# A selective scan on one Trainium2 core: dt * x copied into PSUM by ScalarE, u in PSUM, decays in SBUF three tiles ahead

## The chip, the cores and the metric

The kernel is one program on 1 core of one Trainium2 chip. The metric is the device time of one execution in microseconds (us), as the median of the runs. The core's engines work side by side, each on its own queue of instructions, and wait for one another through semaphores: PE (TensorE, matrix multiplications), DVE (VectorE), ACT (ScalarE), POOL (GpSimd) and SP (SyncE, which here issues all the DMA transfers). SBUF is the large on-chip memory, PSUM the small one of eight banks that PE writes its results to.

## What is computed

The reference runs four layers over 8 images of 56 x 56 positions and 128 channels. Layers 0, 2 and 3 are deformable convolutions with an MLP. Layer 1, the only one that the change touches, is a "visual state space" layer (SS2D): a normalization, a projection to 256 channels and a gate, a 3 x 3 convolution per channel, then a selective scan over the 3136 positions in K = 4 directions with N = 16 states per channel, and after it a normalization, the gate, a projection and an MLP. Of it the scan matters here:

```python
dt = jax.nn.softplus(dt + dt_projs_b[None, :, :, None])
A = -jnp.exp(A_logs).reshape(K, Di, N)

def step(h, t):
    dt_t, u_t, B_t, C_t = t
    h = h * jnp.exp(dt_t[..., None] * A) + (dt_t * u_t)[..., None] * B_t[:, :, None, :]
    y = jnp.einsum('bkdn,bkn->bkd', h, C_t)
    return (h, y)
...
_, ys = jax.lax.scan(step, h0, ts)
```

So for each channel and state there is a decay exp(dt * A), an input (dt * x) * B, a running sum h of decayed inputs, and the output, the sum over the states of h * C.

## The kernel before

**Steps and tiles.** The scan stage of the kernel (`Vss.scans`) goes through 8 images x 4 directions x 4 pieces of 784 positions (SC) = 128 steps. Each step has 32 tiles. A tile (the code's t) holds 32 channels x 4 states on the 128 partitions, and 784 positions; its channel group is cg (8 of them) and its state group sg (0 to 3). All four tiles of one channel group share the load `dt` [128, 2, 784] from DRAM: half 0 is dt, half 1 is dt * x, each channel's row repeated on its four states' partitions. The rows of B and C (`b`, `c`) are loaded once a step and state group. In all there are 4096 tiles and 1024 channel groups.

**One tile.** The operations, with the lines of the profile:

- `spread` (L1340), once per channel group: PE copies dt * x into the PSUM tile `dtu` by multiplying with the identity matrix. There is one buffer of two banks.
- `decay` (L1346): ScalarE writes dA = exp(dt * A) into PSUM, `dA`, two buffers of two banks each.
- `inputs`: for sg = 0, 1, 2 VectorE computes u = dtu * b (L1356) from PSUM into SBUF, `u`, two buffers. For sg = 3 (`on_pool`) GpSimd computes it from SBUF (L1352) into `up`, one buffer.
- the scan (L1449): VectorE's tensor_tensor_scan, h = dA * h + u along the 784 positions, into SBUF, three buffers.
- the state copy (L1452): ScalarE keeps h's last column in `st` for the direction's next piece (not for the last piece).
- `hc` (L1454): GpSimd computes h * c, six buffers.
- `add_sums` (L1378): PE sums over the four states into the PSUM tile `acc`, two tiles at a time and some tiles later; `open_sums` (L1370) and `close_sums` (L1389, ScalarE) begin and end a sum.

VectorE thus does three u and four scans for each channel group, and GpSimd four hc and one up.

**Beside the tiles** run background stages, written as generators that are advanced one piece at a time: `prepare` makes the next step's dt, dt * x, B and C (PE, ScalarE, and two GpSimd operations for each half of the channels), `input_stage` the next image's projections and convolution, `output_stage` the layer's end (with a Gelu or Silu on ScalarE between two loads of its function tables). All matrix results of these go through one PSUM bank, `misc`.

**Order.** In the loop, tile `now` writes down: background pieces, the decay and the u of tile now + 1, at sg = 1 the `spread` of the next channel group, then its own scan, state copy and hc. The tile framework then orders each engine's instructions when the program is built, by a plan of its own with that order as priority, assigns the buffers and adds the semaphore waits. On the chip each engine's queue is in order. `issue_after` puts the state sums behind the last `spread` on PE.

**Memory.** All eight PSUM banks are used: misc 1, dtu 2, dA 2 x 2, acc 1.

Of the kernel before, what the change touches and what calls it, by code (L numbers as in the profile page):

```python
# [41 lines left out]
F32 = mybir.dt.float32  # L42
BF16 = mybir.dt.bfloat16
I32 = mybir.dt.int32
AF = mybir.ActivationFunctionType
ALU = mybir.AluOpType
AX = mybir.AxisListType
PSUM = bass.MemoryType.PSUM
# [70 lines left out]
SC, SR = 784, 14  # L119
NSC = L // SC  # L120
SH = SC // 2
# [11 lines left out]
TC, TS = 32, 4  # L133
NCG, NSG = DI // TC, NST // TS
# [342 lines left out]
class Dcn:  # L477
# [9 lines left out]
    def run(self):  # L487
        tc, nc = self.tc, self.nc
        with ExitStack() as ctx:
            enter = ctx.enter_context  # L490
            self.cp = enter(tc.tile_pool(name="c_const", bufs=1))
            self.img = enter(tc.tile_pool(name="c_img", bufs=1))
            self.fp = enter(tc.tile_pool(name="c_front", bufs=1))
            self.up = enter(tc.tile_pool(name="c_unit", bufs=1))
            self.bp = enter(tc.tile_pool(name="c_block", bufs=3))
            self.tp = enter(tc.tile_pool(name="c_tail", bufs=1))
            self.pt = enter(tc.tile_pool(name="c_pt", bufs=3, space=PSUM))
            self.py = enter(tc.tile_pool(name="c_py", bufs=2, space=PSUM))
            self.pm = enter(tc.tile_pool(name="c_pm", bufs=3, space=PSUM))
            self.w = self.net.dcn_weights(self.layer, self.const)  # L500
            self.constants()
            self.split_bias()
            self.loop()
            self.check()
        over = nc.values_load(self.net.flag[:1, :1], min_val=0, max_val=1, skip_runtime_bounds_check_because="a comparison's result")
        with tc.If(over > 0):
            self.net.dcn_slow(self.layer, self.images, self.src, self.dst)
# [479 lines left out]
        nc.vector.tensor_scalar(net.flag, most, 0.0, None, ALU.is_gt)  # L987


class Vss:  # L990


# [6 lines left out]
    def run(self):  # L999
        tc = self.tc  # L1000
        with ExitStack() as ctx:
            enter = ctx.enter_context
            self.cp = enter(tc.tile_pool(name="v_const", bufs=1))
            self.img = enter(tc.tile_pool(name="v_img", bufs=1))
            self.prep = enter(tc.tile_pool(name="v_prep", bufs=1))
            self.work = enter(tc.tile_pool(name="v_work", bufs=2))
            self.bg = enter(tc.tile_pool(name="v_bg", bufs=1))
            self.dram = enter(tc.tile_pool(name="v_dram", bufs=2, space=DRAM))
            self.pmisc = enter(tc.tile_pool(name="v_misc", bufs=1, space=PSUM))
            self.pdtu = enter(tc.tile_pool(name="v_pdtu", bufs=1, space=PSUM))  # L1010
            self.pda = enter(tc.tile_pool(name="v_pda", bufs=2, space=PSUM))
            self.pacc = enter(tc.tile_pool(name="v_pacc", bufs=1, space=PSUM))
            self.weights()
            self.scans()
# [285 lines left out]
    def scans(self):  # L1300
        nc, w = self.nc, self.w
# [6 lines left out]
        units = [(at, t) for at in range(len(steps)) for t in range(NT)]  # L1308
# [22 lines left out]
        def on_pool(t):  # L1331

            return order[t][1] == NSG - 1

        def spread(at, t):

            s, (cg, sg) = state[at], order[t]
            ps = s["dtu", cg] = self.pdtu.tile([128, 2, 512], F32, name="dtu", tag="dtu")
            for b in range(2):
                last = nc.tensor.matmul(ps[:, b, :SH], lhsT=self.net.ident, rhs=s["dt", cg][:, 1, SH * b : SH * (b + 1)], start=True, stop=True)  # L1340
            self.last_spread = last.ins

        def decay(at, t):
            (i, k, c), s, (cg, sg) = steps[at], state[at], order[t]
            da = s["dA", t] = self.pda.tile([128, 1024], F32, name="dA", tag="dA")
            nc.scalar.activation(da[:, :SC], s["dt", cg][:, 0], AF.Exp, scale=w["A"][:, k, NSG * cg + sg : NSG * cg + sg + 1])  # L1346

        def inputs(at, t):
            s, (cg, sg) = state[at], order[t]
            if on_pool(t):  # L1350
                u = self.work.tile([128, SC], F32, name="up", tag="up", bufs=1)
                nc.gpsimd.tensor_mul(u, s["dt", cg][:, 1], s["b", sg])  # L1352
            else:
                u = self.work.tile([128, SC], F32, name="u", tag="u", bufs=2)
                halves = [v.rearrange("p (x e) -> p x e", x=2) for v in (u, s["b", sg])]
                nc.vector.tensor_mul(halves[0], s["dtu", cg][:, :, :SH], halves[1])  # L1356
            s["u", t] = u
# [13 lines left out]

        def add_sums(at, group):
            acc = state[at]["acc"]
            with self.tc.issue_after(self.last_spread):
                for (cg, sg), hc in group:
                    for b in range(2):
                        r = 64 * b + TC * (cg % 2)
                        nc.tensor.matmul(acc[r : r + TC, :SH], lhsT=w["sum"], rhs=hc[:, SH * b : SH * (b + 1)], start=False, stop=sg == NSG - 1)  # L1378

        def close_sums(at, t):  # L1380
            (i, k, c), acc, (h, r) = steps[at], state[at]["acc"], place(t)
# [15 lines left out]
                    tasks.extend(self.output_stage(i, e) for e in (2 * c + 1, 2 * c))  # L1397

        spread(*units[0])
        decay(*units[0])  # L1400
        inputs(*units[0])
        st = ready = None
        group, late = [], deque()
        zeros = self.zeros()
        for now, (at, t) in enumerate(units):
            (i, k, c), s, (cg, sg) = steps[at], state[at], order[t]
            forward = k < 2
            if t == 0:
                if at % NSC == 0:
                    st = self.prep.tile([128, NT], F32, name="st", tag="st", bufs=2)  # L1410
                    nc.gpsimd.memset(st, 0.0)
                if at % (NDIR * NSC) == 0 and i + 1 < self.images:
                    tasks.append(self.input_stage(i + 1))
                ready = iter(())
                if at + 1 < len(steps):
                    if steps[at + 1][0] > i:
                        self.load_xb(i + 1)
                    ready = self.prepare(state[at + 1], *steps[at + 1][1:])
            if t % (2 * NSG) == 0:
                late.append((now + 5, open_sums, (at, t)))  # L1420
            while late and late[0][0] <= now:
                _, do, args = late.popleft()
                do(*args)
            if t % 2 == 0:
                next(ready, None)

            if sg == 1:
                to = divmod(NCG * at + cg + 2, NCG)
                if to[0] < len(steps):
                    self.fetch_dt(state[to[0]], to[1])  # L1430
            if t in (3, 19):
                next(zeros, None)

            for x, when in enumerate(((25, 28, 29, 30), (26, 29, 30, 31))):
                if t in when and at + 1 < len(steps):
                    self.fetch_row(state[at + 1], x, when.index(t))
            if now + 1 < len(units):
                decay(*units[now + 1])
                if not on_pool(units[now + 1][1]):
                    inputs(*units[now + 1])  # L1440

                if sg == NSG - 3 and now + 3 < len(units):
                    spread(*units[now + 3])
            if now + 2 < len(units) and on_pool(units[now + 2][1]):
                inputs(*units[now + 2])
            hh = self.work.tile([128, SC], F32, name="h", tag="h", bufs=3)
            step = 1 if forward else -1
            u, dA = s.pop(("u", t)), s.pop(("dA", t))
            nc.vector.tensor_tensor_scan(hh[:, ::step], dA[:, :SC][:, ::step], u[:, ::step], st[:, t : t + 1], ALU.mult, ALU.add)  # L1449
            if c != (NSC - 1 if forward else 0):  # L1450
                last = SC - 1 if forward else 0
                nc.scalar.copy(st[:, t : t + 1], hh[:, last : last + 1])  # L1452
            hc = self.work.tile([128, SC], F32, name="hc", tag="hc", bufs=6)
            nc.gpsimd.tensor_mul(hc, hh, s["c", sg])  # L1454
            group.append((order[t], hc))
            if t % 2:
                late.append((now + 3, add_sums, (at, group)))
                group = []
                if t % (2 * NSG) == 2 * NSG - 1:
                    late.append((now + 5, close_sums, (at, t)))  # L1460
            if t % 2 or t % 4 == 0 or (i == self.images - 1 and k == 2):
                advance(1)
# [81 lines left out]
```

## Time and profile before

| what | value |
|---|---|
| median of 3 runs | 18469.42 us (18464.81 to 18477.36) |
| profiled execution, span | 18479.8 us |
| the scan stage in it, first to last scan | 2376 to 13812 us, 11436 us |
| busy over the whole span: PE, DVE, ACT, POOL | 13780.6, 15510.8, 11145.4, 11801.5 us |
| busy in the scan stage: PE, DVE, ACT, POOL | 8635.2, 10255.6, 7049.6, 10451.1 us |
| granted TensorE clock, mean | 0.826 |

The profile is of one execution. The span counts from the first to the last instruction, and has no launch around it; it is 10.4 us above the median of the timed runs. A row of the profile's groups names a line of the kernel, an engine, the operation, what it writes and reads, how often it ran, its busy time and the mean of one in ns, and behind the last bar the idle time of that engine ahead of it with what ended most of that idle time. In a row of the timeline stand the start and the duration of one instruction; the last part of an instruction can overlap the next one's start on the same engine.

### The profile page before, as it was taken

How to read it: one execution, taken by the hardware profiler on the slowest of the kernel's cores; microseconds unless marked ns; L12 is line 12 of the kernel's file. 1: busy time of each engine (PE TensorE's matmuls, PEld its weight loads, DVE VectorE, ACT ScalarE, POOL GpSimd, SP SyncE). 2: the span in 40 equal slices, each digit the busy share in tenths (PEclk: the TensorE clock that was granted, in tenths of full speed). 3: DMA queues.
4: the chain of work that ended last, by engine and by line, in shares of the span. 5: the costliest groups of instructions: out<-in, count | busy, mean ns of one | idle time of the engine just before them, and what ended most of it. 6: DMA issues, size and time to landing. Idle time of an engine off the chain costs nothing. (4 is left out here: it accounts for less than half of the span.)

```text
span 18479.8 us, 257190 instructions
## 1 busy us (share of the span) xinstructions
PE 13780.6 (75%) x89795; PEld 6844.2 (37%) x89795; DVE 15510.8 (84%) x18797; ACT 11145.4 (60%) x20690; POOL 11801.5 (64%) x6462
## 2 busy tenths in 40 slices
PE   5777787678678778678778768767665888577777
PEld 4555422222222222222222222222224666455555
DVE  8888379988988988988988898898985887688886
ACT  4666565566566566566566656656554666456666
POOL 2221089998998998998998998899981111222221
PEclk7878888889889889889888888888886888677777
DMA  7777444444443444344343443443433777577777
GB/s 215 205 210 200 122 158 160 162 158 148 142 149 137 146 147 140 140 150 139 140 150 136 143 152 135 143 150 136 147 122 110 196 198 198 143 204 204 201 204 175
DMA packets 1341779, 2961.90 MB, mean 160 GB/s; under 512 B 91168, under 2 KB 892132, under 8 KB 1325836
## 3 DMA queue, kind: packets, MB, share of 16 engines
q1 hardware_dynamic: 1340460, 2945.21, 51.4%
q8 instruction: 718, 11.76, 0.3%
q14 instruction: 601, 4.92, 0.1%
HBM read 2243.88 MB, written 866.92 MB: 168 GB/s over the span
## 5 line engine op out<-in xcount | busy, mean ns | idle before, releaser
L1454 POOL TENSOR_TENSOR hc<-h,c 128x784 f32<-128x784 f32 x4096 | 7560.9, 1873 | 764.2 <-DVE h L1449 534.4
L1449 DVE TENSOR_TENSOR_SCAN h<-dA,st,u 128x784 f32<-128x784 f32 x3072 | 5569.9, 1838 | 316.2 <-ACT dA L1346 182.3
L1346 ACT ACTIVATE dA<-dt,v_A 128x784 f32<-128x784 f32 x4096 | 3742.8, 915 | 719.1 <-DVE h L1449 717.8
L1356 DVE TENSOR_TENSOR u<-dtu,b 128x784 f32<-128x784 f32 x3072 | 2875.7, 957 | 559.9 <-PE dtu L1340 555.5
L1378 PE MATMUL acc<-hc,v_sum 128*32 128x392 f32 x16384 | 3222.3, 552 | 105.8 <-POOL hc L1454 105.6
L1340 PE MATMUL dtu<-dt,ident 128*128 128x392 f32 x4096 | 2105.1, 642 | 1512.1 <-issue 1102.6
L736 POOL TENSOR_TENSOR ay<-hat,om 112x756 f32<-112x756 f32 (+2 forms) x192 | 525.8, 2738 | 2750.0 <-ACT hat L727 2346.6
L1449 DVE TENSOR_TENSOR_SCAN h<-dA,st,up 128x784 f32<-128x784 f32 x1024 | 1876.7, 1833 | 242.4 <-POOL hc L1454 176.7
L1352 POOL TENSOR_TENSOR up<-dt,b 128x784 f32<-128x784 f32 x1024 | 1900.3, 1856 | 132.1 <-DVE h L1449 110.8
L807 ACT COPY st<-pt 128x448 f32<-128x448 f32 (+1 forms) x2240 | 1177.8, 542 | 1216.4 <-PE pt L805 1210.1
L1452 ACT COPY st<-h 128x1 f32<-128x1 f32 x3072 | 581.7, 189 | 2159.0 <-DVE h L1449 2150.5
L1340 PEld LDWEIGHTS dtu<-dt,ident 128*128 128x128 f32 x4096 | 862.0, 235 | 2564.6 <-issue 1672.2
L775 DVE TENSOR_TENSOR win<-win,patch 112x252 f32 (+2 forms) x3456 | 1695.4, 503 | 124.4 <-DVE win L775 34.2
L805 PE MATMUL pt<-ident,sw 112*128 112x112 f32 (+2 forms) x8960 | 1609.7, 310 | 199.1 <-DMA sw<-skew 198.8
L1378 PEld LDWEIGHTS acc<-hc,v_sum 128*32 128x32 f32 x16384 | 769.8, 117 | 2488.2 <-issue 1675.4
L766 POOL MEMSET win<- 128x1820 f32 (+2 forms) x384 | 630.1, 1646 | 1466.2 <-DMA skew<-win 1159.6
L821 PE MATMUL yps<-st,xw 128*32 128x48 f32 (+5 forms) x35840 | 1077.7, 245 | 397.6 <-ACT st L807 394.8
L805 PEld LDWEIGHTS pt<-ident,sw 112*128 112x128 f32 (+2 forms) x8960 | 1119.5, 161 | 485.6 <-DMA sw<-skew 166.9
L772 DVE TENSOR_TENSOR patch<-ay,hat 112x756 f32<-112x756 f32 (+2 forms) x1152 | 1221.3, 1066 | 22.5 <-POOL ay L736 19.5
L821 PEld LDWEIGHTS yps<-st,xw 128*32 128x32 f32 (+2 forms) x35840 | 757.0, 126 | 825.9 <-ACT st L807 476.1
L1112 PE MATMUL misc<-xn,v_tap 128*128 128x448 f32 x2016 | 867.3, 574 | 96.5 <-ACT xn L1146 61.2
L725 ACT ACTIVATE hat<-om,taps 112x252 f32<-112x252 f32 x1280 | 755.7, 729 | 287.1 <-DVE patch L772 273.4
(165 smaller groups left out, 19517.2 us busy)
## 6 DMA issues: line engine op xcount, KB each, us to landing
dt<-dds SPq DMA_DIRECT2D x1024, 784.0 KB
b<-rows SPq DMA_DIRECT2D x512, 392.0 KB
c<-rows SPq DMA_DIRECT2D x512, 392.0 KB
dds<-dd SPq DMA_DIRECT2D x256, 784.0 KB
sw<-skew SPq DMA_DIRECT2D x224, 812.0 KB
sw<-skew SPq DMA_DIRECT2D x224, 672.0 KB
sw<-skew SPq DMA_DIRECT2D x224, 588.0 KB
xw<-table SPq DMA_DIRECT2D x224, 320.0 KB
```

What stands on the lines that cost most here:

```text
L772: nc.vector.tensor_mul(patch[:n], bcast(a, 3, KX), bcast(b, 2, KY))
L775: self.last_add = nc.vector.tensor_add(to, to, patch[:n, NCB * p : NCB * (p + 1)]).ins
L805: last = nc.tensor.transpose(ps[:m, n * g : n * (g + 1)], sw[:n, g, p : p + m], self.net.ident[:n, :n])
L807: nc.scalar.copy(st[:m], ps[:m, : G * n])
L821: self.nc.tensor.matmul(yps[CG * g : CG * (g + 1), t0:t1], lhsT=xw[:m, k + part, CG * g : CG * (g + 1)], rhs=st[:m, at + t0 : at + t1], st ...
L1340: last = nc.tensor.matmul(ps[:, b, :SH], lhsT=self.net.ident, rhs=s["dt", cg][:, 1, SH * b : SH * (b + 1)], start=True, stop=True)
L1346: nc.scalar.activation(da[:, :SC], s["dt", cg][:, 0], AF.Exp, scale=w["A"][:, k, NSG * cg + sg : NSG * cg + sg + 1])
L1352: nc.gpsimd.tensor_mul(u, s["dt", cg][:, 1], s["b", sg])
L1356: nc.vector.tensor_mul(halves[0], s["dtu", cg][:, :, :SH], halves[1])
L1378: nc.tensor.matmul(acc[r : r + TC, :SH], lhsT=w["sum"], rhs=hc[:, SH * b : SH * (b + 1)], start=False, stop=sg == NSG - 1)
L1449: nc.vector.tensor_tensor_scan(hh[:, ::step], dA[:, :SC][:, ::step], u[:, ::step], st[:, t : t + 1], ALU.mult, ALU.add)
L1454: nc.gpsimd.tensor_mul(hc, hh, s["c", sg])
```

## The change

- `spread`: a ScalarE copy of dt * x (both halves in one instruction) into `dtu` takes the place of the two identity matmuls, and is written down at sg = 2, for the next channel group, where it was at sg = 1. The state sums are no longer held behind it on PE.
- `decay`: for sg = 0, 1, 2 dA goes to SBUF, four buffers; for sg = 3 to PSUM, one buffer of its own (`dAp`). All are written down three tiles ahead (AHEAD) where it was one.
- `inputs`: VectorE's u goes to PSUM, one buffer of two banks, and is written down in its own tile just ahead of its scan, where it was one tile ahead in two SBUF buffers. GpSimd's `up` stays as it was, two tiles ahead.
- PSUM is again full: misc 1, dtu 2, dAp 2, u 2, acc 1.
- The scratch ring of descriptors for DMAs that GpSimd issues is set to 8192 bytes, half its size.

```diff
+AHEAD = 3
...
-            self.pda = enter(tc.tile_pool(name="v_pda", bufs=2, space=PSUM))
+            self.pda = enter(tc.tile_pool(name="v_pda", bufs=1, space=PSUM))
+            self.pu = enter(tc.tile_pool(name="v_pu", bufs=1, space=PSUM))
...
             ps = s["dtu", cg] = self.pdtu.tile([128, 2, 512], F32, name="dtu", tag="dtu")
-            for b in range(2):
-                last = nc.tensor.matmul(ps[:, b, :SH], lhsT=self.net.ident, rhs=s["dt", cg][:, 1, SH * b : SH * (b + 1)], start=True, stop=True)
-            self.last_spread = last.ins
+            nc.scalar.copy(ps[:, :, :SH], s["dt", cg][:, 1].rearrange("p (b e) -> p b e", b=2))
...
-            da = s["dA", t] = self.pda.tile([128, 1024], F32, name="dA", tag="dA")
-            nc.scalar.activation(da[:, :SC], s["dt", cg][:, 0], AF.Exp, scale=...)
+            if on_pool(t):
+                da = s["dA", t] = self.pda.tile([128, 1024], F32, name="dAp", tag="dAp")[:, :SC]
+            else:
+                da = s["dA", t] = self.work.tile([128, SC], F32, name="dA", tag="dA", bufs=4)
+            nc.scalar.activation(da, s["dt", cg][:, 0], AF.Exp, scale=...)
...
-                u = self.work.tile([128, SC], F32, name="u", tag="u", bufs=2)
+                u = self.pu.tile([128, 1024], F32, name="u", tag="u")[:, :SC]
...
-            with self.tc.issue_after(self.last_spread):
-                for (cg, sg), hc in group:
+            for (cg, sg), hc in group:
...
         spread(*units[0])
-        decay(*units[0])
-        inputs(*units[0])
+        for x in range(AHEAD):
+            decay(*units[x])
...
-            if now + 1 < len(units):
-                decay(*units[now + 1])
-                if not on_pool(units[now + 1][1]):
-                    inputs(*units[now + 1])
-
-                if sg == NSG - 3 and now + 3 < len(units):
-                    spread(*units[now + 3])
+            if now + AHEAD < len(units):
+                decay(*units[now + AHEAD])
+            if not on_pool(t):
+                inputs(at, t)
+            if sg == NSG - 2 and now + 2 < len(units):
+                spread(*units[now + 2])
             if now + 2 < len(units) and on_pool(units[now + 2][1]):
                 inputs(*units[now + 2])
...
-    nc = bacc.Bacc("TRN2", target_bir_lowering=False, num_devices=1)
+    nc = bacc.Bacc("TRN2", target_bir_lowering=False, num_devices=1, dynamic_dma_scratch_size=8192)
```

More of the change, by code (lines that the diff above doesn't have):

```diff
@@ L1338, in spread @@
             ps = s["dtu", cg] = self.pdtu.tile([128, 2, 512], F32, name="dtu", tag="dtu")
-            for b in range(2):
-                last = nc.tensor.matmul(ps[:, b, :SH], lhsT=self.net.ident, rhs=s["dt", cg][:, 1, SH * b : SH * (b + 1)], start=True, stop=True)
-            self.last_spread = last.ins
+            nc.scalar.copy(ps[:, :, :SH], s["dt", cg][:, 1].rearrange("p (b e) -> p b e", b=2))
         def decay(at, t):
             (i, k, c), s, (cg, sg) = steps[at], state[at], order[t]
-            da = s["dA", t] = self.pda.tile([128, 1024], F32, name="dA", tag="dA")
-            nc.scalar.activation(da[:, :SC], s["dt", cg][:, 0], AF.Exp, scale=w["A"][:, k, NSG * cg + sg : NSG * cg + sg + 1])
+            if on_pool(t):
+                da = s["dA", t] = self.pda.tile([128, 1024], F32, name="dAp", tag="dAp")[:, :SC]
+            else:
+                da = s["dA", t] = self.work.tile([128, SC], F32, name="dA", tag="dA", bufs=4)
+            nc.scalar.activation(da, s["dt", cg][:, 0], AF.Exp, scale=w["A"][:, k, NSG * cg + sg : NSG * cg + sg + 1])
         def inputs(at, t):
@@ L1373, in add_sums @@
             acc = state[at]["acc"]
-            with self.tc.issue_after(self.last_spread):
-                for (cg, sg), hc in group:
-                    for b in range(2):
-                        r = 64 * b + TC * (cg % 2)
-                        nc.tensor.matmul(acc[r : r + TC, :SH], lhsT=w["sum"], rhs=hc[:, SH * b : SH * (b + 1)], start=False, stop=sg == NSG - 1)
+            for (cg, sg), hc in group:
+                for b in range(2):
+                    r = 64 * b + TC * (cg % 2)
+                    nc.tensor.matmul(acc[r : r + TC, :SH], lhsT=w["sum"], rhs=hc[:, SH * b : SH * (b + 1)], start=False, stop=sg == NSG - 1)
         def close_sums(at, t):
@@ L1448, in scans @@
             u, dA = s.pop(("u", t)), s.pop(("dA", t))
-            nc.vector.tensor_tensor_scan(hh[:, ::step], dA[:, :SC][:, ::step], u[:, ::step], st[:, t : t + 1], ALU.mult, ALU.add)
+            nc.vector.tensor_tensor_scan(hh[:, ::step], dA[:, ::step], u[:, ::step], st[:, t : t + 1], ALU.mult, ALU.add)
             if c != (NSC - 1 if forward else 0):
```

## The prediction

> **What bounds the kernel now.** I read the busy time by stage first, then, for the scan stage alone, the groups by line, VectorE's waits, its timeline, and the critical chain's last pieces.
>
> The scan stage runs from the first scan at 2376 us to 13812 us, and all that the change touches lies in it:
>
> ```profile
> core 0: us, PE busy (x) PEld busy (x) DVE busy (x) ACT busy (x) POOL busy (x), PEclk, DMA share, GB/s
> 2376.00:13812.00 11436.00, 8635.16 (x31301) 3029.64 (x31300) 10255.58 (x8597) 7049.57 (x13024) 10451.07 (x5761) 0.86 0.41 145
> ```
>
> GpSimd is busy for 10451 of 11436 us and VectorE for 10256, so neither has 10% to spare; ScalarE has 4386 us free. The groups of that stage:
>
> ```profile
> L1454 POOL TENSOR_TENSOR hc<-h,c 128x784 f32<-128x784 f32 x4093 | 7555.5, 1873 | 761.2 <-DVE h L1449 531.4 <-PE acc L1378 176.1 <-DMA gate<-pre 13.4
> L1449 DVE TENSOR_TENSOR_SCAN h<-dA,st,u 128x784 f32<-128x784 f32 x3069 | 5564.4, 1838 | 316.1 <-ACT dA L1346 182.3 <-POOL hc L1454 37.7 <-issue 16.6
> L1346 ACT ACTIVATE dA<-dt,v_A 128x784 f32<-128x784 f32 x4090 | 3737.4, 915 | 719.1 <-DVE h L1449 717.8 <-ACT st L1452 0.5
> L1356 DVE TENSOR_TENSOR u<-dtu,b 128x784 f32<-128x784 f32 x3067 | 2871.1, 957 | 477.9 <-PE dtu L1340 473.5
> L1340 PE MATMUL dtu<-dt,ident 128*128 128x392 f32 x4088 | 2099.1, 642 | 1510.3 <-issue 1102.6 <-DVE u L1356 379.0 <-PE misc L1090 6.7
> ```
>
> GpSimd waits mostly for scans, scans for decays, u for dtu. VectorE's own longest waits:
>
> ```profile
> DVE u L1356 <- PE dtu L1340: 473.5, 258, 7.8
> DVE h L1449 <- ACT dA L1346: 234.3, 199, 4.2
> DVE h L1449 <- POOL hc L1454: 214.4, 165, 3.2
> ```
>
> (Total us, times, longest us.) VectorE's timeline shows a cost that is in no wait list:
>
> ```profile
> 8128.86 0.95 DVE L1356 TENSOR_TENSOR u<-dtu,b 128x784 f32<-128x784 f32 x1
> 8129.72 1.84 DVE L1449 TENSOR_TENSOR_SCAN h<-dA,st,u 128x784 f32<-128x784 f32 x1
> ...
> 8181.05 0.95 DVE L1356 TENSOR_TENSOR u<-dtu,b 128x784 f32<-128x784 f32 x1
> 8182.13 1.85 DVE L1449 TENSOR_TENSOR_SCAN h<-dA,st,u 128x784 f32<-128x784 f32 x1
> ```
>
> At 8129.72 a scan follows a u that it does not need: it starts 0.86 us after that u, before u's 0.95 us are over. At 8182.13 it needs the u just ahead: 1.08 us. Over the stage's VectorE rows the overlap of independent pairs is 0.084 us, and the gap where a scan takes the u just ahead 0.133 us: 0.217 us dearer. Where an instruction has only VectorE's own predecessor to wait for (the convolution chain of L637, the layer norm's last operations) the gap is 0.035 us, 0.118 us dearer.
>
> **The change part by part.** The sum is made against the profiled span, 18479.8 us; the median of the runs, 18469.4, lies 10.4 below it, which I take off at the end.
>
> *dtu from ScalarE.* 4096 matmuls of 642 ns (2099 us of PE) and their weight loads go, and 1024 copies come to ScalarE. The nearest rows are the two plain 128x784 operations of L1268 and L1269, 855 and 848 ns, and the decay, 915 ns: 0.85 us each, 870 us in all, so ScalarE goes from 7050 to 7920 us, 69% of the stage. The 473 us of VectorE waiting for dtu go, and what is late next is ScalarE itself. The copy can start when the group's third u is done; VectorE then has a scan and the GpSimd-fed scan to do, 3.6 us, so the copy must begin within 2.65 us. How late ScalarE is for something VectorE has just released can be read from the state copy L1452: of 3072 it began over 2.65 us after its scan's end in 224, and the excess is 86 us per 1024. With 12% more on the engine I take 100 (ends: 0, and the present 473). Net -373. Behind the waiting copy ScalarE holds the next decays, the state copies and the background stages; the decays are ahead, so I charge nothing more here, and the second rival prices it.
>
> *Decays three tiles ahead.* VectorE's 234 us for dA nearly vanish: three tiles are some 8 us of cover, and the longest wait was 4.2. I leave 30 (ends 0 and 234): net -204. Writing SBUF instead of PSUM costs ScalarE at most some 0.03 us per decay (855 without a per-partition scale against 915 with one into PSUM), off the path. The dt buffers are both released and needed two tiles earlier; a dt load lands in 4.7 us median, 14.1 at worst of 500, against some 11 us or more: nothing. The fourth decay keeps one PSUM buffer, free when the previous GpSimd-fed scan ends, a group earlier: nothing.
>
> *u in one PSUM buffer, issued beside its scan.* This is the cost. Now u may run ahead, as two SBUF buffers allow; the commonest order between two GpSimd-fed scans is u u scan scan u scan (565 of 1024 groups), with one direct hand-off. With one buffer u must be followed by its scan, and the next u may not start before that scan has read the buffer: u waits on VectorE's own semaphore for this today too, only two scans back. So 3072 hand-offs u to scan at 0.217 us, and 2048 from scan to u at 0.118 us (the first u of a group has the GpSimd-fed scan between). Background operations stand behind u in 15% of cases and behind a scan in 6% today; I let them hide as much: 567 + 227 = 794 us. Already paid: 565 x 0.217 + 106 x 0.118 = 135. Net +659 (ends: 0, and 774 with nothing hidden). The Trainium skill, "VectorE: DVE Perf Modes", section "The DRAIN you can't avoid", says that a chain of copies with a semaphore after each took as long as one with a semaphore at the end; by it this term would be 0 and the sum some 17,890. The 0.86 and 1.08 us above disagree, and I go by them.
>
> *u's duration.* No VectorE operation in this trace writes PSUM. Nearest rows: the statistics operation reading PSUM (417 ns for 256 columns) and SBUF (270 for 128) differ by some 13 ns once their slope is out; at the far end, the convolution's 128x784 all in SBUF is 1057 ns against u's 957. I take +13 ns x 3072 = +40 us, ends -307 and +307. The scan keeps one PSUM and one SBUF operand, exchanged: nothing. "Perfetto Trace Analysis", section "Optimizing Scalar/DVE Operations", gives VectorE about 60 ns of overhead per instruction on SBUF and 125 on PSUM, which speaks against moving u; by it the term would be an estimated 200 us. No run here shows it yet.
>
> *The rest.* VectorE's 218 us for GpSimd (hc and up) come in bursts when GpSimd prepares the next step, which stays: -30 (ends -218 and 0). Its 99 us for PE in background operations (48 statistics, 51 residual adds) profit from the freed PE: -15 (ends -99 and 0). The ring: every DMA was issued from SP and all of its packets are hardware_dynamic, so a smaller GpSimd ring is touched by nothing: 0; only the slow fallback path, which has no row, would use it.
>
> Sum: -373 - 204 + 659 + 40 - 30 - 15 = +77; 18479.8 + 77 - 10.4 = 18546.
>
> **The rivals.** The forecast is a small difference of two large terms, so I give the other ways much room. A measurement of this kernel tells some 0.2%, 37 us, from no change: 18432 to 18507 counts as the same.
>
> *Faster: the hand-off hardly costs.* With dA ready early, the GpSimd-fed scan may be planned between a u and its scan, and a hand-off through PSUM may be quicker than through SBUF. For it: the planner already moves u's freely, and the waits of 473 and 234 us are certain to be attacked. Against: three u's and one such scan per group. Decisive point: a net hand-off term under 582 us. At half my term, 18546 - 330 = 18216; at none, 17887.
>
> *Slower: ScalarE takes PE's place.* Its copy waits at the head of an in-order queue, with 4 us blocks (a Gelu of 1.51 us between two table loads of 1.28) near. If the present 473 and 234 come back in full, +577: 19123; at half, 18835. Against: the state copy's lateness above.
>
> *Slower: PSUM is dear for VectorE.* At 100 ns per u, 267 us over my 40: 18813.
>
> *Nothing.* GpSimd at 91% sets the pace whatever VectorE does, or the new waits equal the old: 18470.
>
> **How the numbers follow.** Forecast (slower by 0.2 to 1.3%) 0.32, its own range 18507 to 18710; ScalarE 0.10; PSUM 0.08; nothing 0.13; hand-off cheap 0.37. Slower is 0.32 + 0.10 + 0.08 = 0.50, same 0.13, faster 0.37. The range 18160 to 18950 takes in the faster rival down to 0.6 of my hand-off term gone (386 of 659 us), and the two slower ones at their middle values, and leaves some 0.1 out at the bottom and 0.07 at the top.
>
> **What would show it.** Right: no PE dtu row; VectorE's wait for dtu, now on ScalarE, near 100 us; dA waits near 30; the u row at some 970 ns; u to scan start near 1.08 us in most tiles, and VectorE busy plus short gaps some 700 us up. GpSimd's busy time stays at 10451. Wrong: scans starting 0.87 us behind their own u (the first rival); waits on ScalarE of several hundred us (the second); u over 1050 ns (the third). A change outside the scan stage would contradict all of this.

## The result, and the profile after

The changed kernel took 18813.6 us (median; 18803.5 to 18815.1), the kernel before 18467.1: 1.0185 times as long, 95% interval 1.0171 to 1.0199. The forecast was 18546, so the sign was right and the size was not: +346 us where +77 was given.

The profiled execution has a span of 18801.9 us, 322 more than before. All of it lies in the scan stage. (By the timeline the first scan starts and the last one ends at 2366 and 13800 us before, at 2363 and 14123 after: the windows of the views, before and after, begin and end some 10 us late, and their lengths hold.) The stage's busy times (columns as before):

```profile
core 0: us, PE busy (x) PEld busy (x) DVE busy (x) ACT busy (x) POOL busy (x), PEclk, DMA share, GB/s
2373.00:14134.00 11761.00, 8314.35 (x27236) 2315.37 (x27232) 10613.33 (x8608) 7823.57 (x14051) 10420.19 (x5760) 0.75 0.40 141
```

GpSimd has the same work as before (10420 us) and more idle time around it. VectorE's busy time has grown by 358 us, and the granted clock of PE has fallen from 0.86 to 0.75 although PE has less to do. The groups that answer to those shown of before:

```profile
L1457 POOL TENSOR_TENSOR hc<-h,c 128x784 f32<-128x784 f32 x4093 | 7515.6, 1855 | 1181.9 <-DVE h L1452 1040.8 <-PE acc L1382 57.5 <-DVE bn_mv L1074 30.4
L1452 DVE TENSOR_TENSOR_SCAN h<-dA,st,u 128x784 f32<-128x784 f32 x3069 | 5661.1, 1845 | 347.2 <-POOL hc L1457 21.0 <-ACT st L1455 14.3 <-DVE u L1361 2.8
L1382 PE MATMUL acc<-hc,v_sum 128*32 128x392 f32 x16378 | 4486.8, 651 | 2007.6 <-POOL hc L1457 1998.0
L1361 DVE TENSOR_TENSOR u<-dtu,b 128x784 f32<-128x784 f32 x3069 | 2988.4, 974 | 389.5 <-ACT dtu L1343 328.5
L1343 ACT COPY dtu<-dt 128x784 f32<-128x784 f32 x1022 | 832.9, 815 | 29.2 <-DVE u L1361 25.7
```

u costs 974 ns, the copy 815, the decays into SBUF 944 (914 into PSUM). The line to stop at is L1382: the state sums' matmuls, 552 ns each before, take 651, and PE sits idle for 2000 us ahead of them waiting for hc; before, that idle time was 106 us:

```profile
L1378 PE MATMUL acc<-hc,v_sum 128*32 128x392 f32 x16376 | 3220.1, 552 | 105.8 <-POOL hc L1454 105.6
```

VectorE's waits (total us, times, longest):

```profile
DVE u L1361 <- ACT dtu L1343: 328.5, 184, 5.3
DVE xt L1231 <- PE misc L1228: 134.9, 50, 5.3
DVE xt L1202 <- PE misc L1199: 119.6, 46, 8.8
DVE bn_st L1073 <- PE misc L1177: 91.1, 63, 5.0
DVE h L1452 <- POOL hc L1457: 60.6, 91, 2.2
```

The wait for decays is gone (3 us in all). That for dtu went down by only 145, and three waits for PE's background results, 99 us together before, make 346. VectorE's timeline over one channel group:

```profile
8024.10 0.98 DVE L1361 TENSOR_TENSOR u<-dtu,b 128x784 f32<-128x784 f32 x1 [2.79 <-ACT dtu L1343]
8025.19 1.85 DVE L1452 TENSOR_TENSOR_SCAN h<-dA,st,u 128x784 f32<-128x784 f32 x1
8027.07 0.98 DVE L1361 TENSOR_TENSOR u<-dtu,b 128x784 f32<-128x784 f32 x1
8028.18 1.85 DVE L1452 TENSOR_TENSOR_SCAN h<-dA,st,u 128x784 f32<-128x784 f32 x1
8030.06 0.98 DVE L1361 TENSOR_TENSOR u<-dtu,b 128x784 f32<-128x784 f32 x1
8031.18 1.85 DVE L1452 TENSOR_TENSOR_SCAN h<-dA,st,u 128x784 f32<-128x784 f32 x1
8032.94 1.82 DVE L1452 TENSOR_TENSOR_SCAN h<-dAp,st,up 128x784 f32<-128x784 f32 x1
```

The order is u, scan, u, scan, u, scan and the GpSimd-fed scan in all 1024 groups. In these lines u and its scan are 1.09 to 1.12 us apart from start to start, and the next u starts 1.88 us after the scan. And this is how the 2.79 us ahead of the first u came about (ScalarE and PE in the same stretch):

```profile
8017.28 0.84 PE L1382 MATMUL acc<-hc,v_sum 128*32 128x392 f32 x2 [2.44 <-POOL hc L1457]
8018.06 0.42 PE L1094 MATMUL misc<-ident,z 98*128 98x98 f32 x1
8018.41 1.52 PE L1382 MATMUL acc<-hc,v_sum 128*32 128x392 f32 x2
8019.86 0.43 PE L1094 MATMUL misc<-ident,z 98*128 98x98 f32 x1
...
8020.32 0.68 ACT L1212 ACTIVATE xT<-misc,v_col 128x392 f32<-128x392 f32 x1 [5.06 <-PE misc L1094]
...
8022.76 0.59 ACT L1218 ACTIVATE pre<-misc,v_col 128x392 f32<-128x392 f32 x1 [0.83 <-PE misc L1217]
8023.25 0.82 ACT L1343 COPY dtu<-dt 128x784 f32<-128x784 f32 x1
```

PE stands at a state sum for 2.44 us because hc is not there. The background transposes (L1094) stand behind and between the sums. ScalarE waits 5.06 us for the last of them and, for a product made from it (L1217), another 0.83; the copy of dtu stands behind both on ScalarE, and VectorE waits for the copy. Three engines in a row wait for GpSimd's hc, which only the sum needs.

VectorE's stage before and after, in us (path = busy time and gaps under 0.15 us):

| | before | after | difference | forecast |
|---|---|---|---|---|
| path (hand-offs and u's duration) | 10347 | 10986 | +639 | +699 |
| wait for dtu | 473 | 328 | -145 | -373 |
| wait for dA | 234 | 3 | -231 | -204 |
| wait for PE's background results | 99 | 346 | +247 | -15 |
| wait for GpSimd | 218 | 64 | -154 | -30 |
| DMA, state copy, other | 67 | 36 | -31 | 0 |
| sum | | | +325 | +77 |

The stage grew by 326 us, so the table is complete. The two rows that missed are the second and the fourth; the experiments are about these.

### The profile page after: what moved, and what is told of

Its sections match the earlier page's. It is cut to its first block, busy times and chain, and to the rows that moved or that the text cites. A ratio compares the mean times of both kernels' runs of the same rounds, so it can differ in the third digit from the quotient of the medians.

```text
span 18801.9 us, 249197 instructions
## 1 busy us (share of the span) xinstructions
PE 13456.7 (72%) x85699; PEld 6131.5 (33%) x85699; DVE 15871.6 (84%) x18797; ACT 11921.0 (63%) x21714; POOL 11774.0 (63%) x6462
## 5 line engine op out<-in xcount | busy, mean ns | idle before, releaser
L1457 POOL TENSOR_TENSOR hc<-h,c 128x784 f32<-128x784 f32 x4096 | 7521.1, 1855 | 1181.9 <-DVE h L1452 1040.8
L1452 DVE TENSOR_TENSOR_SCAN h<-dA,st,u 128x784 f32<-128x784 f32 x3072 | 5666.7, 1845 | 347.5 <-POOL hc L1457 21.0
L1382 PE MATMUL acc<-hc,v_sum 128*32 128x392 f32 x16384 | 4489.4, 651 | 2012.3 <-POOL hc L1457 2002.6
L1361 DVE TENSOR_TENSOR u<-dtu,b 128x784 f32<-128x784 f32 x3072 | 2991.3, 974 | 467.8 <-ACT dtu L1343 406.6
L1351 ACT ACTIVATE dA<-dt,v_A 128x784 f32<-128x784 f32 x3072 | 2895.2, 944 | 268.4 <-DVE h L1452 237.3
L1382 PEld LDWEIGHTS acc<-hc,v_sum 128*32 128x32 f32 x16384 | 785.9, 124 | 5422.0 <-POOL hc L1457 4164.9
L1357 POOL TENSOR_TENSOR up<-dt,b 128x784 f32<-128x784 f32 x1024 | 1899.5, 1855 | 70.5 <-DVE h L1452 69.3
L1452 DVE TENSOR_TENSOR_SCAN h<-dAp,st,up 128x784 f32<-128x784 f32 x1024 | 1870.0, 1826 | 63.3 <-POOL hc L1457 39.6
L1351 ACT ACTIVATE dAp<-dt,v_A 128x784 f32<-128x784 f32 x1024 | 935.5, 914 | 86.0 <-DVE h L1452 85.4
L1375 PE MATMUL acc<-y,ident 128*64 128x392 f32 x1536 | 595.3, 810 | 460.8 <-ACT y L1393 333.3
L1393 ACT COPY y<-acc 64x392 f32<-64x392 f32 x768 | 574.9, 749 | 534.8 <-PE acc L1382 526.7
```

What stands on the lines that cost most here:

```text
L1351: nc.scalar.activation(da, s["dt", cg][:, 0], AF.Exp, scale=w["A"][:, k, NSG * cg + sg : NSG * cg + sg + 1])
L1452: nc.vector.tensor_tensor_scan(hh[:, ::step], dA[:, ::step], u[:, ::step], st[:, t : t + 1], ALU.mult, ALU.add)
```

## The experiments

Three theories of why PE's results and the copy come late: A, PE's clock, which fell with the removed matmuls; B, ScalarE's own load and queue; C, the order of PE's queue, since the state sums are no longer held behind a spread. Half-rate time is the part of the scan stage in which the profile's clock records grant PE half its speed. All times are medians; the kernel before measured 18467 to 18480 us beside each, so a difference of some 15 us between two kernels says nothing.

**fill1: give PE its work back, without a new wait.** The added matmul reads an hc that the sums behind it wait for anyway; `none` holds zeros.

```diff
+            (cg, _), hc = group[0]
+            for x in range(1):
+                r = 64 * (x % 2) + TC * (cg % 2)
+                nc.tensor.matmul(acc[r : r + TC, :SH], lhsT=w["none"], rhs=hc[:, SH * (x % 2) : SH * (x % 2 + 1)], start=False, stop=False)
             for (cg, sg), hc in group:
```

> The changed kernel with one more state-sum matmul per two tiles (zero weights, same hc, same acc rows): 2048 matmuls, as many as the identity matmuls that the change took from PE, with no new wait. Theory A, the clock: without the identity matmuls PE falls to half rate for 5827 us of the scan stage instead of 3202, so PE-fed work comes late, VectorE waits for misc (346 us instead of 99) and ScalarE waits for misc with the dtu copy behind it (VectorE waits 328 us for dtu). With the filler half-rate time goes back towards 3200 us, the state-sum matmul's mean from 651 to near 555 ns, VectorE's misc wait under 170, its dtu wait under 200; time 18460 to 18600. Theory B, ScalarE's queue is late by its own load, whatever PE's clock: the clock may rise, but the waits stay; 18770 to 18850. Theory C, PE's queue order (sums waiting for hc ahead of background work): more PE work in that queue makes it worse, above 18830.

18845.9 us, 1.0199 (1.0182 to 1.0216). The clock came back: half-rate time some 3400 us (5820 in the changed kernel, 3200 before), the sum's matmul at 570 ns. The waits did not go: 317 us for dtu, 283 for misc. Theory A, which gave under 200, under 170 and at most 18600 us, falls; the time lies in the ranges of both B and C. GpSimd's results also held VectorE up more (193 us for hc), and nothing was gained.

```profile
DVE u L1363 <- ACT dtu L1345: 317.3, 187, 7.7
DVE h L1458 <- POOL hc L1463: 192.6, 140, 7.4
DVE bn_st L1075 <- PE misc L1179: 96.5, 52, 7.1
```

**pe_spread: undo the copy alone.**

```diff
-            nc.scalar.copy(ps[:, :, :SH], s["dt", cg][:, 1].rearrange("p (b e) -> p b e", b=2))
+            for b in range(2):
+                nc.tensor.matmul(ps[:, b, :SH], lhsT=self.net.ident, rhs=s["dt", cg][:, 1, SH * b : SH * (b + 1)], start=True, stop=True)
```

> The changed kernel with the two identity matmuls back in place of ScalarE's copy; u in PSUM, decays in SBUF three ahead and all positions stay. Theory A: half-rate time back near 3200 us and the misc waits near 100; dtu waits now on PE, 200 to 470 us; the VectorE path (busy plus short gaps 10979 us) stays; 18600 to 18850. Theory B: ScalarE is relieved of 833 us, so what waited for it goes, 18450 to 18600. If the hand-offs were no cost, it would be at 18100 or less.

19685.5 us, 1.065 (1.0632 to 1.0668), far above every expectation. VectorE waits 1412 us for dtu on PE, three times as long as in the kernel before with the same matmuls. What this kernel has not of the kernel before, besides u, the decays, the spread's place in the program and the ring, is the hold of the sums behind them. This brought theory C to the front.

**copy_only: the copy alone, in the kernel before.**

```diff
-            for b in range(2):
-                last = nc.tensor.matmul(ps[:, b, :SH], lhsT=self.net.ident, ...)
-            self.last_spread = last.ins
+            nc.scalar.copy(ps[:, :, :SH], s["dt", cg][:, 1].rearrange("p (b e) -> p b e", b=2))
...
-            with self.tc.issue_after(self.last_spread):
-                for (cg, sg), hc in group:
+            for (cg, sg), hc in group:
```

> The kernel before with ScalarE's copy alone (u in two SBUF buffers, decays in PSUM one ahead as before; sums not held behind the spread). Theory A: the clock falls as in the changed kernel (half rate for 5500 us or more), VectorE's misc waits rise to some 350 us, its dtu wait on ScalarE is some 330, dA 234 or more, the path keeps its 10338 us: 18467 - 473 + 330 + 250 = 18574, 18480 to 18680. Theory B (ScalarE's load): dtu and dA waits above 600 us together, misc waits unchanged, similar time. If both are wrong and the hand-offs are all of the loss: 18150 to 18350.

18685.8 us, 1.0109 (1.0092 to 1.0126): over half of the loss is there without any of the new hand-offs (path 10336 us). The time is just above theory A's range. VectorE waits 679 us for dA, 176 for dtu and 227 for misc: theory B had the first two above 600 us together, but misc unchanged. With decays only one tile ahead it is the decay that is behind on ScalarE.

**copy_fill: the same with the filler.** The edits of copy_only and fill1 together.

> The kernel before with ScalarE's copy and the zero-weight filler of 2048 matmuls. Theory A: the clock stays near that of the kernel before, misc waits near 100 us, dtu on ScalarE 100 to 200: 18467 - 473 + 150 = 18144, 18100 to 18300, faster than both kernels. Theory B: as copy_only within 60 us. Theory C: slower than copy_only.

18876.8 us, 1.0212 (1.0195 to 1.0229): the clock restored (half rate some 3610 us) and 191 us slower than without the filler. With fill1 this settles A: at a better clock, more matmuls in PE's queue gave nothing there and did harm here.

**before_nohold: the kernel before without its hold.**

```diff
-            with self.tc.issue_after(self.last_spread):
-                for (cg, sg), hc in group:
+            for (cg, sg), hc in group:
```

> The kernel before with only the hold taken away: the state sums are no longer put behind the last identity matmul on PE. Theory C, PE's queue order: planned early, the sums wait for hc at the head of PE's queue, and the identity matmuls and background work stand behind them. PE's idle time ended by hc rises from some 750 us to over 3000, VectorE's wait for dtu from 473 to over 900 us; 18850 to 19500. Theory B, ScalarE's own load and queue: nothing changes there, 18420 to 18540. Theory A, the clock, has fallen with the filler run and expects no change either.

19401.2 us, 1.0502 (1.0485 to 1.052), within theory C's range; theory B had seen no change. One line is worth 922 us, at a granted clock of 0.821 against 0.825, so the clock can have little part in them. VectorE's wait for dtu, 473 us in the kernel before, and the idle time of PE and its weight loads ahead of all operations on acc (us, times; in the kernel before, and then in this one; the idle times of matmuls and weight loads are added, so one stretch can count twice):

```profile
DVE u L1356 <- PE dtu L1340: 1361.3, 634, 10.0
```

```profile
POOL hc L1454: 754.5, 882
```

```profile
POOL hc L1453: 5301.1, 3370
```

In the changed kernel that last number is 6156.6 us. So the changed kernel carries the same fault; ScalarE's copy, which need not pass PE's queue, hides the greater part of it.

**late4: write the sums down one tile later.**

```diff
-                late.append((now + 3, add_sums, (at, group)))
+                late.append((now + 4, add_sums, (at, group)))
```

> The changed kernel with the state sums written down four tiles after their second hc instead of three (one number). Theory C: PE waits less for hc at the head of its queue, so background matmuls come earlier, ScalarE waits less for them, and the dtu copy behind comes earlier: VectorE's misc waits from 346 to under 200 us, dtu from 328 to under 200; 18480 to 18650. Part of it may come back as GpSimd waiting for a free hc buffer (57 us now). Theory B: as the changed kernel, 18780 to 18850.

18796.9 us, 1.0171 (1.0154 to 1.0188), within the changed kernel's interval, and every wait as there (dtu 324, misc 357 us). The edit changes the place in the program's text, and that is only a priority to the planner: PE's idle time ended by hc hardly moved either (5844 us against 5918 in the same window). It is no test of theory C, which needs an order, not a priority.

**pe_hold: identity matmuls and hold back, u and decays as changed.**

```diff
-            nc.scalar.copy(ps[:, :, :SH], s["dt", cg][:, 1].rearrange("p (b e) -> p b e", b=2))
+            for b in range(2):
+                last = nc.tensor.matmul(ps[:, b, :SH], lhsT=self.net.ident, ...)
+            self.last_spread = last.ins
...
-            for (cg, sg), hc in group:
+            with self.tc.issue_after(self.last_spread):
+                for (cg, sg), hc in group:
```

> The changed kernel with the identity matmuls on PE and the hold behind them, both as in the kernel before; u in PSUM and decays in SBUF three ahead stay. Theory C: against 19686 us without the hold, VectorE's dtu wait falls from 1412 to some 300 to 600 us; with its path 640 us longer than before and the dA waits gone: 18700 to 18950. Theory B, which sees no part for the hold: 19500 to 19700.

18864.9 us, 1.0209 (1.0192 to 1.0226): 821 us less than pe_spread by the hold alone, the dtu wait from 1412 back to 475 us. Against the kernel before it also gives the price of u in PSUM and the early decays (with the spread's later place and the ring) under the old hold: 386 us.

**u2: take the hand-offs away.** Two PSUM buffers for u, written a tile ahead; all decays in SBUF to make room.

```diff
-            self.pda = enter(tc.tile_pool(name="v_pda", bufs=1, space=PSUM))
-            self.pu = enter(tc.tile_pool(name="v_pu", bufs=1, space=PSUM))
+            self.pu = enter(tc.tile_pool(name="v_pu", bufs=2, space=PSUM))
...
-            if not on_pool(t):
-                inputs(at, t)
-            if sg == NSG - 2 and now + 2 < len(units):
-                spread(*units[now + 2])
+            if now + 1 < len(units) and not on_pool(units[now + 1][1]):
+                inputs(*units[now + 1])
+            if sg == NSG - 3 and now + 3 < len(units):
+                spread(*units[now + 3])
```

> The changed kernel with two PSUM buffers for u, written one tile ahead as before; the decay of the GpSimd-fed tile goes to SBUF to make room (four decay buffers for all tiles), and the copy stands one tile earlier. It takes the hand-offs away: VectorE's busy time plus short gaps from 10986 to some 10400 us. If hand-offs set the time: 18250 to 18500. If the waits for dtu and PE's results take over what is freed: 18650 to 18800. The GpSimd-fed scan now reads two SBUF operands: its row, 1826 ns, and hc's, 1855, show whether the two engines hinder each other; if they do, by some 0.5 us a tile, 500 us come back.

19721.3 us, 1.0674 (1.0656 to 1.0692): the hindrance between VectorE and GpSimd that was named as a possibility is large and covers what was to be measured.

```profile
L1449 DVE TENSOR_TENSOR_SCAN h<-dA,st,u 128x784 f32<-128x784 f32 x3069 | 5555.2, 1832 | 416.6 <-POOL hc L1454 220.3 <-ACT st L1452 61.7 <-ACT dA L1347 36.1
L1449 DVE TENSOR_TENSOR_SCAN h<-dA,st,up 128x784 f32<-128x784 f32 x1023 | 3040.5, 2972 | 294.4 <-POOL hc L1454 197.5 <-ACT st L1452 85.4 <-ACT dA L1347 8.2
```

The scan with both operands in SBUF takes 2972 ns, with one in PSUM 1832; GpSimd's hc rose from 1855 to 2007 ns. The operands alone do not do it: the 70 of these scans during which GpSimd was wholly idle took 1815 to 1853 ns. The short gaps did fall, from 365 to 96 us, but the kernel says nothing of the hand-offs' whole price.

**after_sth: the changed kernel with a hold of another kind.** The sums are put behind a one-column matmul that adds zero and waits for a later state copy.

```diff
+            mark = nc.tensor.matmul(acc[r : r + TC, :1], lhsT=w["none"], rhs=st[:, col : col + 1], start=False, stop=False)
+            with self.tc.issue_after(mark.ins):
...
-                late.append((now + 3, add_sums, (at, group)))
+                late.append((now + 3, add_sums, (at, group, (t + 2) % NT)))
```

> The changed kernel with a hold for the state sums in another form: ahead of each group of sums stands a one-column matmul with zero weights that reads the state copy of the tile three further on (so it waits for ScalarE's copy after that scan, in the three of four pieces that have one), and the sums are put behind it on PE. Theory C, PE's queue order: PE no longer stands at sums whose hc is not there (5918 us of its idle time in the changed kernel), background matmuls come earlier, ScalarE waits less for PE, VectorE's misc waits fall from 346 towards 150 us and dtu from 328 towards 150: 18400 to 18650. If the wait on ScalarE's copy only takes the place of the wait for hc at the head of PE's queue: 18780 to 19000. Theory B, ScalarE's own load: 18780 to 18850.

18552.3 us, 1.0038 (1.0024 to 1.0052): 261 us of the 346 are gone, as theory C gave, and against the kernel before only 72 are left. VectorE's waits:

```profile
DVE u L1363 <- ACT dtu L1345: 218.0, 159, 5.0
DVE xt L1204 <- PE misc L1201: 125.9, 39, 11.4
DVE xt L1233 <- PE misc L1230: 66.9, 31, 3.9
DVE h L1456 <- POOL hc L1461: 60.5, 83, 1.4
DVE bn_st L1075 <- PE misc L1179: 51.4, 52, 3.1
```

PE's idle time ahead of acc operations is now ended by the state copy in 3307 us and by hc in 1309 (6157 in the changed kernel). So PE still waits, but for another event, and VectorE's waits for background results went from 346 to 244 us. That the background matmuls now stand ahead of the waiting sums fits this, but was not counted.

**copy_sth: the copy and the same hold, in the kernel before.** The edits of copy_only and after_sth.

> The kernel before with ScalarE's copy and the same hold behind the state copy (u in SBUF, decays in PSUM one ahead). Theory C: against 18686 us without a hold, the dA waits fall from 678 towards 250 us and dtu stays near 150, with the path of the kernel before (10338 us): 18100 to 18400, faster than both kernels. If the marker's wait replaces the wait for hc: 18600 to 18900.

18349.0 us, 0.9929 (0.9913 to 0.9946), within theory C's range and faster than both kernels, by 0.7% and 2.5%. dA waits 421 us, dtu 161, path 10339.

**after_stha: the hold in all four pieces.** On top of after_sth:

```diff
-            if c != (NSC - 1 if forward else 0):
+            if True:
                 last = SC - 1 if forward else 0
                 nc.scalar.copy(st[:, t : t + 1], hh[:, last : last + 1])
```

> The changed kernel with the hold behind the state copy, and the state copy made after every scan, so that the hold works in all four pieces of a direction instead of three (1024 copies of 0.19 us more on ScalarE). Theory C: PE's idle time ended by hc falls from 1263 us further towards the 753 of the kernel before; VectorE's waits for dtu and misc, 218 and 244 us, fall by a quarter of what the hold brought (262 us in three quarters, so some 80): 18440 to 18530. If ScalarE's extra copies cost as much: 18530 to 18620.

18447.7 us, 0.9984 (0.9974 to 0.9993): the whole of the changed kernel's loss is gone. dtu wait 109 us, misc 214, path 10990. PE's idle time ahead of acc operations is now ended by hc in 56 us and by the state copy in 4305: PE waits, but no longer for GpSimd.

**copy_stha: copy_sth with the same.**

> The kernel before with ScalarE's copy and the same hold after every scan. Theory C: 18349 us without the hold in the fourth piece; the three quarters brought 337 us against no hold, so some 110 more: 18210 to 18330. If ScalarE's extra copies cost as much: 18340 to 18420.

18248.8 us, 0.988 (0.9863 to 0.9896), the fastest: 1.2% under the kernel before, 3.0% under the changed one. Its stage:

```profile
core 0: us, PE busy (x) PEld busy (x) DVE busy (x) ACT busy (x) POOL busy (x), PEclk, DMA share, GB/s
2368.00:13570.00 11202.00, 7928.63 (x31351) 2764.46 (x31349) 10265.14 (x8612) 7869.38 (x15097) 10452.27 (x5768) 0.80 0.42 149
```

VectorE's and GpSimd's work is that of the kernel before, in a run 228 us shorter, at a PE clock of 0.80 against 0.86. VectorE's wait for dtu is 137 us, for dA 302.

**All together** (us):

| spread, hold of the sums | u in SBUF, decays in PSUM | u in PSUM, decays early | difference |
|---|---|---|---|
| PE, held behind it | 18479 (before) | 18865 | +386 |
| PE, not held | 19401 | 19686 | +285 |
| ScalarE, not held | 18686 | 18814 (after) | +128 |
| ScalarE, held in three pieces of four | 18349 | 18552 | +203 |
| ScalarE, held in all | 18249 | 18448 | +199 |

## Why the prediction was wrong in size

**The step that failed is the one that was not there.** The change's description said that the state sums are no longer held behind the spread, and the prediction gave that no price: it stands in no term and in no rival. It showed in two terms: VectorE's wait for dtu, taken at 100 us, was 328, and its wait for PE's background results, taken to fall by 15 us, rose by 247. Its rival "ScalarE takes PE's place" had the place right (the copy at the head of an in-order queue, and what stands before it) but sought the reason in ScalarE's own blocks. ScalarE's load was not the reason: with the full hold (after_stha) the same copy on a ScalarE that does more (7946 us against 7830) waits VectorE out for 109 us, not 328. The forecast of 100 for this wait came from how late the state copy was in the kernel before, which had the hold. It fits a held kernel and could not be carried to one that is not: read in the same way, the state copy's lateness (what it began beyond 2.65 us after its scan's end) is 86 us per 1024 before, 226 in the changed kernel and 82 in after_stha.

**"A smaller PE load helps the background": wrong in sign.** -15 was given, +247 measured; 214 remain with the full hold. PE had 321 us less to do and its background results came later, because what decided here is not PE's load but what stands at the head of its queue.

**The hand-offs: right as VectorE's path.** Mechanism, place and size: +639 us of path against +699. Without the 17 ns per u and the 7 ns per scan some 570 us are left for the hand-offs, where 659 were taken. The pieces: the gap from u to its scan is 0.134 us where the scan also waits for a decay and 0.104 where it does not (0.133 was taken for all), the gap from a scan to the next u 0.034. The Trainium skill, "VectorE: DVE Perf Modes", section "The DRAIN you can't avoid", has a semaphore after each operation of a chain of copies cost nothing extra. Short gaps of 365 us in the changed kernel against 82 before say otherwise here. Background operations hid 17% behind u where 15% was taken (2546 of 3072 u's have their scan as the next row), and some 15% between a scan and the next u where 6% was. The rival in which the hand-off hardly costs is out as a mechanism. In time the hand-offs were not priced alone: with the early decays they cost 386 us under the old hold and 199 with the copy and the new one.

**u into PSUM: right.** 974 ns against 957, +17 where +13 was taken. "Perfetto Trace Analysis", section "Optimizing Scalar/DVE Operations", would have given an estimated 65 ns more by its two overheads; the trace does not show them here. The scan of these tiles went from 1838 to 1845 ns with its operands exchanged.

**Decays: right**, 3 us of wait left where 30 was given. Into SBUF they take 944 ns, into PSUM 914, the 0.03 us that was given, though the two rows named for it (855 ns into SBUF, 915 into PSUM) do not yield it. **VectorE's waits for GpSimd** fell by 154 where 30 was given; a likely reason, not tested, is that a slower VectorE does not catch up with GpSimd's bursts. **The copy** took 815 ns (850 taken).

**The weighing.** The likeliest case and the faster rival together had 0.69 of the chance, both resting on the hand-off alone. That the rival "PSUM is dear for VectorE" had 18813, the measured time, is chance: u became 17 ns longer, not 100. The kernel with a full hold takes 18448 us, 98 below the forecast of 18546. There the path (+643 us), the wait for dtu (-364) and that for dA (-230) come within 60 us of their terms each; background results (+115 against -15) and GpSimd (-148 against -30) miss by more and cancel in good part, so the nearness of the sum is partly luck. The unpriced hold is worth 366 us, from 18814 to 18448, by a hold of another kind than the one that was taken away.

**What stays open.** The hold also raised the granted clock (0.75 to 0.80 in the stage); how much of the 366 us this makes, and what a hold at the clock of the kernel before would give, was not tried. The early decays and the halved ring were not run alone; no DMA is issued from GpSimd in either trace. Nor is it shown how far a hold can be improved beyond the state copy: 214 us of VectorE's waits for PE remain in after_stha.

## What to carry to other kernels

A line that only orders instructions has a price like any other: when a change removes the instruction that an ordering hangs on, list what the ordering kept from standing at the head of the queue, and price it. On in-order queues planned at build time look for a chain of three: a consumer planned too early waits at the head of one queue, background work behind it is late, and a second engine waits for that with its own urgent work behind; the giveaway is an engine with much idle time and late results at once. Keep a producer and its consumer on the same engine apart by one instruction where buffers allow it: here, each direct pair cost 0.12 to 0.22 us.

## What had not been expected of the hardware

PE's clock went down when work was taken from PE: half-rate time in the stage rose from some 3200 to 5820 us when the 2048 identity matmuls (4096 rows of the trace) went, and fell back to 3400 with as many zero-weight matmuls put in. Yet the clock did not set the time: with the filler one kernel was no faster (18846 against 18814 us) and the other 191 us slower, and the fastest kernel here ran at 0.80 where the kernel before had 0.86. And two SBUF operands on VectorE beside a GpSimd that is busy most of the time cost a scan of 1.83 us another 1.14 on average, and nothing while GpSimd was idle.
